# Softmax sums over the partitions inside the layer-1 stages: a transposing reduce on VectorE in place of products with ones on TensorE

## Chip, cores and metric

The kernel runs on one core of a Trainium2 chip. The metric is the device time of one execution in microseconds (us). Every time quoted is a median of runs in the fast state (none more than 1.5% above the fastest of its kernel), unless it is called a profiled span, which is the length of the one execution that the hardware profiler recorded. Six names of engines appear in the profile: PE is TensorE's matmuls, PEld its weight loads, DVE is VectorE, ACT is ScalarE, POOL is GpSimd, and SP is the engine that issues the transfers.

## What is computed

Eight images of 64 channels and 64x64 places pass through two attention layers. In both, every place attends to all 4096 places of its image, and the softmax divides by a sum over all keys. All is fp32.

```python
# layer 0: 8 channels of f and g, 64 of h
s = einsum('bci,bcj->bij', f, g)
o = einsum('bcj,bij->bci', hh, softmax(s, axis=2))
x = x + o
# layer 1: group norm, then q, k, v with 64 channels each
attn = softmax(einsum('bqc,bkc->bqk', q, k) * c ** -0.5)
out = w_proj @ einsum('bqk,bkc->bqc', attn, v) + b_proj
x = out + x
```

## The kernel before

The stages follow one another as layer 0 of image 0, layer 0 of image 1, layer 1 of image 0, layer 0 of image 2, layer 1 of image 1 and so on, each of four chunks of queries. A chunk has 16 steps. A record is one matmul as the profile lists it; an fp32 product appears as two (the four products of one sum are eight records). One step of layer 1 is a group of 16 scores records on TensorE, their exponentials `e` on ScalarE, and a group of 16 that weighs the values by `e` and adds into two accumulators. VectorE adds every `e` into `esum`. The eight PSUM banks are two accumulators (0 and 7) and three pairs that are handed out in turn:

```python
pairs = [banks[:, 2 * k + 1 : 2 * k + 3, :] for k in range(3)]
outer = (0, 7)
def pair():
    ...
    turn += 1
    return pairs[turn % 3]
```

When a chunk has ended, `esum` still holds, on each of 128 partitions, partial sums over different keys. They have to be added over the partitions. Before the change this is done for all of the 64 chunks but the last, so 63 times, by products of a matrix of ones with `esum`:

```python
def finish(self, acc, esum, c, index):
    copied = self.total(raw, acc)       # VectorE copies the accumulators out (layer 1)
    vector.tensor_add(esum[:, 0], esum[:, 0], esum[:, 1])        # 128x1024 is left

    def sums(spare):
        z = banks[:, spare, :] if spare is not None else pair()[:, 0, :]
        for h in range(2):
            for i in range(2):
                row = 32 * (2 * h + i)
                matmul(z[row : row + 32, 0:width], ones[:, 0:32], esum[:, 0, h, ts(i, width)],
                       start=True, stop=True, tile_position=(0, row))
        nc.scalar.copy(zs, z[:, 0:width])
        ...                              # four transfers: one row each, to 32 rows of zt

    def reciprocals():
        vector.reciprocal(rt, zt)        # 128x8, then through HBM to a row for all channels
    ...
# some steps also make a chunk of values for a later stage (64x64 products into a pair);
# VectorE copies them out to vt, which frees the pair
# who runs when: `delay` steps after the end of the chunk
delay = 7 if at.kind == 0 else 5
at_step(now + delay, lambda: sums(spare), PAIR if spare is None else BANK)
at_step(steps[0], behind(reciprocals), 0)        # 3 or 4 steps later; after most layer-0 chunks, in the next layer-1 stage
at_step(steps[1], behind(result), 0)
```

If the next chunk is one of layer 0, the products go to a spare outer bank; inside layer 1 they take a pair in its turn.

Of the kernel before, what the change touches and what calls it, by code (L numbers as in the profile page):

```python
# [9 lines left out]
F32 = mybir.dt.float32  # L10
# [3 lines left out]
ALU = mybir.AluOpType  # L14
AX = mybir.AxisListType
# [5 lines left out]
P = 128  # L21
# [47 lines left out]
def fast_path(  # L69
# [19 lines left out]
    nc = tc.nc  # L89
# [3 lines left out]
    NC = NH // CW  # L93
# [8 lines left out]
    work = ctx.enter_context(tc.tile_pool(name="work", bufs=2))  # L102
# [6 lines left out]
    banks = psum.tile([P, 8, CW], F32, name="banks")  # L109
    pairs = [banks[:, 2 * k + 1 : 2 * k + 3, :] for k in range(3)]  # L110
    outer = (0, 7)
# [3 lines left out]
    def pair():  # L115
        nonlocal turn
        if lent is not None:
            return pairs[lent]
        turn += 1
        return pairs[turn % 3]  # L120
# [26 lines left out]
    vector = InOrder()  # L147

    def matmul(*args, **kwargs):
        in_order(nc.tensor.matmul(*args, **kwargs))  # L150
# [96 lines left out]
    QP = 2 * CW // P  # L247
# [65 lines left out]
    class Attention:  # L313
# [26 lines left out]
        def finish(self, acc, esum, c, index):  # L340

            n = f"{self.name}_{c}"
            raw = work.tile([P, CW], F32, tag="raw", bufs=4, name=f"raw_{n}")
            copied = self.total(raw, acc)
            zt = small.tile([P, QP], F32, tag="zt", bufs=4, name=f"zt_{n}")
            width = CW // 2
            with tc.issue_after(copied.ins if self.kind == 1 else added):
                vector.tensor_add(esum[:, 0], esum[:, 0], esum[:, 1])
            r = None

            def sums(spare):

                if spare is not None:
                    z = banks[:, spare, :]
                else:
                    z = pair()[:, 0, :]

                zs = work.tile([P, width], F32, tag="zs", name=f"zs_{n}")
                for h in range(2):
                    for i in range(2):  # L360
                        row = 32 * (2 * h + i)
                        matmul(
                            z[row : row + 32, 0:width], ones[:, 0:32], esum[:, 0, h, ts(i, width)],
                            start=True, stop=True, tile_position=(0, row),
# [5 lines that stand above are left out]
                        nc.sync.dma_start(zt[row : row + 32, :], zs[row : row + 1, :])  # L370

            def broadcast():
                nonlocal r
                r = work.tile([P, CW], F32, tag="r", name=f"r_{n}")

            def reciprocals():
                rt = stash[:, ts(index, QP)]
                vector.reciprocal(rt, zt)
                broadcast()
                dealt = recips[index]  # L380
                nc.sync.dma_start(dealt, rt)
                for h in range(2):
                    row = dealt[ts(h, C), :].rearrange("p e -> (p e)")
                    nc.sync.dma_start(r[ts(h, C), :], row.partition_broadcast(C))

            def result():
                vector.tensor_mul(raw, raw, r)
                self.residual(raw, c)

            return sums, reciprocals, result  # L390

        def end(self, acc, esum, e, t):

# [49 lines left out]
    class Layer0(Attention):  # L443
        kind = 0
        scale = 1.0
        banks = 1
# [121 lines left out]
    class Layer1(Attention):  # L568
        kind = 1
        scale = C**-0.5  # L570
        banks = 2
# [130 lines left out]
    PAIR, BANK = 1, 2  # L702

    def at_step(s, work_, takes=PAIR):
        nonlocal count
        later.append((s, count, work_, takes))
        later.sort(key=lambda u: u[:2])
        count += 1
# [29 lines left out]
    added = None  # L738
# [20 lines left out]
    def weigh(i, j, e, cols, now):  # L759
        nonlocal acc, esum, first, added  # L760
        at, c = seq[i]
        t, p = divmod(j, 2)
        n = f"{at.name}_{c}"
        if j == 0 and cols.start == 0:
            acc = [banks[:, outer[(c + m) % 2 if at.kind == 0 else m], :] for m in range(at.banks)]
            esum = work.tile([P, 2, 2, CW], F32, tag="esum", name=f"esum_{n}")
        at.weigh(acc, e[:, p], t, p, j == 0, j == 2 * NT - 1, cols)
        if p == 0 or cols.stop < CW:
            return
        if t == 0:  # L770
            first = e
        else:
            added = vector.tensor_add(esum, first if t == 1 else esum, e).ins
        if t == NT - 1:
            finished(i, now)

    def finished(i, now):

        nonlocal closed
        at, c = seq[i]  # L780
        closed = max(closed, 1)
        next_kind = seq[i + 1][0].kind if i + 1 < len(seq) else 1
        works = at.finish(acc, esum, c, i)
        sums, reciprocals, result = works
        delay = 7 if at.kind == 0 else 5
        spare = None
        if next_kind == 0:

            spare = outer[c % 2 if at.kind == 0 else 1]
        if at.kind == 1 and c < NC - 1:  # L790
            spare = None

        at_step(now + delay, lambda: sums(spare), PAIR if spare is None else BANK)

        layer1 = (i // NC + 1) * NC * NT
        if at.kind == 0 and at.b > 0 and c < NC - 1:
            when = layer1 + 1 + 2 * c
            steps = (when, when + 3)
        else:

            wait = 4 if next_kind == 0 else 3
            steps = (now + delay + wait, now + delay + 2 * wait)


        def behind(work_):
            def made():
                with tc.issue_after(added):
                    work_()

            return made  # L810

        at_step(steps[0], behind(reciprocals), 0)
        at_step(steps[1], behind(result), 0)
# [31 lines left out]
    i = 0  # L845
    while i < len(seq):
        at, c = seq[i]
        tight = i < 2 * NC
        if at.kind == 1:
            for j in range(0, 2 * NT, 2):  # L850
                now = i * NT + j // 2
# [21 lines left out]
        while u < len(units):  # L873
            k, t = units[u][:2]
            now = k * NT + t
# [19 lines left out]
            while group:  # L895
# [3 lines left out]
                at, c = seq[k]  # L899
# [12 lines left out]
        i = last  # L912
    now = len(seq) * NT
# [390 lines left out]
```

## Time and profile before

| | before |
|---|---|
| median of 3 runs | 3076.77 us (3076.73 to 3078.01) |
| profiled span, granted TensorE clock | 3076.1 us, 0.998 |
| TensorE, VectorE, ScalarE busy | 99%, 82%, 66% |
| one layer-1 stage, one layer-0 stage | 231.84 us, 147.12 us |

The page's busy line says which engine has no time left, the chain that ended last says whether it also sets the end, and the windows give the same busy times for one stage. What a group costs is read from the timeline, by the differences of starts: matmul groups overlap (in the prediction's timeline groups of 1.97 us start 1.72 us apart), so their durations do not add up. The prediction below shows those views. One more line of the page belongs to the start, the group of the products with ones; its columns are engine, operation, result and operands, shapes, count, then busy us and mean ns of one, then the idle time ahead of them and what ended it.

```profile
L150 PE MATMUL banks<-esum_l,ones 128*32 128x256 f32 x520 | 41.3, 391 | 1.6 <-DVE vt_l L140 1.6
```

These 520 records are 63 sums of 4 products in 2 records each, and 16 records of the last chunk. By this line all 63 sums seem to cost some 40 us. By the starts, the 32 sums that the change touches cost 26.8 us alone.

### The profile page before, as it was taken

To read this page: it belongs to the slowest core of one execution; us is meant where nothing else is said; L and a number is where in the kernel's file an instruction comes from. 1 tells how busy PE (TensorE), PEld (TensorE's weight loads), DVE (VectorE), ACT (ScalarE), POOL (GpSimd) and SP (SyncE) were. 2 spreads that over 40 slices of the span, in tenths; PEclk is the share of its full clock that TensorE was granted. 3 is DMA by queue.
4 is the path that set the end of the run, shared out by engine and by line. 5 is a ranking of instruction groups with operands and counts; after the bars stand their busy time and mean duration, and the time that the engine had idled before them with its cause. 6 is when DMAs were issued, how large, how long until landed. Compare 5 with 4: busy or idle time off the path is not lost.

```text
span 3076.1 us, 59457 instructions
## 1 busy us (share of the span) xinstructions
PE 3047.3 (99%) x26113; PEld 1133.4 (37%) x26113; DVE 2533.3 (82%) x1604; ACT 2045.4 (66%) x2004; POOL 16.4 (1%) x45
## 2 busy tenths in 40 slices
PE   8999999999999999999999999999999999999998
PEld 3333334333343333433334333343333333333433
DVE  6999876899768987689877898779987799876666
ACT  6878655786557865578555785558855588555554
POOL 2000000000000000000000000000000000000000
PEclk9999999999999999999999999999999999999999
DMA  3000010100101001010011000100001000000000
GB/s 78 22 8 12 19 39 15 32 1 15 39 22 25 1 15 39 22 25 1 15 39 26 22 1 18 40 21 22 1 25 36 19 8 1 15 22 15 9 15 13
DMA packets 57531, 62.54 MB, mean 20 GB/s; under 512 B 30816, under 2 KB 30864, under 8 KB 57264
## 3 DMA queue, kind: packets, MB, share of 16 engines
q1 hardware_dynamic: 56272, 58.51, 7.7%
q8 instruction: 206, 3.38, 0.5%
q14 instruction: 61, 0.50, 0.1%
q0 software_dynamic: 672, 0.12, 0.0%
q10 hardware_dynamic: 320, 0.04, 0.0%
HBM read 25.06 MB, written 8.65 MB: 11 GB/s over the span
## 4 chain that ended last, share of the span: by engine, by line
PE 94%; DVE 4%; ACT 1%; issue 1%; DMA 0%; SPq 0%; DVEq 0%; ACTq 0%
PE banks L150 94%; DVE esum_l L140 3%; ACT e_l L902 0%; ACT e_l L861 0%; DVE vt_l L140 0%; DMA x<-in_x_dram 0%; ACT full_l L526 0%; DVE rt L140 0%; DVE w_l L140 0%; DVE x L140 0%; SPq L179 0%; DVE raw_l L140 0%; DVE st_l L140 0%; DVE raw_end L140 0%; DVE guess_l L140 0%
## 5 line engine op out<-in xcount | busy, mean ns | idle before, releaser
L140 DVE TENSOR_TENSOR esum_l<-esum_l,e_l 128x2048 f32<-128x2048 f32 x895 | 2050.2, 2291 | 453.3 <-ACT e_l L861 403.6
L861 ACT ACTIVATE e_l<-banks 128x1024 f32<-128x1024 f32 x1024 | 993.0, 1022 | 800.1 <-PE banks L150 777.8
L150 PE MATMUL banks<-e_l,v_l 64*64 64x512 f32 (+2 forms) x8772 | 1100.4, 588 | 0.0
L902 ACT ACTIVATE e_l<-banks 128x512 f32<-128x512 f32 (+3 forms) x767 | 957.0, 1311 | 193.8 <-PE banks L150 178.2
L150 PE MATMUL banks<-kq_l 64*64 64x512 f32 (+1 forms) x8448 | 1009.5, 586 | 3.4 <-ACT e_l L902 3.2
L150 PE MATMUL banks<-e_l,vt_l 128*64 128x512 f32 (+1 forms) x4060 | 831.7, 550 | 0.0
L150 PEld LDWEIGHTS banks<-e_l,v_l 64*64 64x64 f32 (+1 forms) x8772 | 362.0, 133 | 573.4 <-issue 526.4
L150 PEld LDWEIGHTS banks<-kq_l 64*64 64x64 f32 (+1 forms) x8448 | 348.2, 134 | 578.3 <-issue 542.3
L150 PEld LDWEIGHTS banks<-e_l,vt_l 128*64 128x64 f32 x4060 | 266.9, 136 | 471.4 <-issue 451.4
L150 PE MATMUL banks<-fg_l 32*128 32x512 f32 x1792 | 210.8, 460 | 6.4 <-ACT e_l L902 4.1
L150 PEld LDWEIGHTS banks<-fg_l 32*128 32x128 f32 x1792 | 85.8, 182 | 189.6 <-ACT e_l L902 138.3
L140 DVE TENSOR_TENSOR esum_l<-e_l,e_l 128x2048 f32<-128x2048 f32 x64 | 146.3, 2286 | 6.5 <-ACT e_l L861 6.5
L140 DVE TENSOR_TENSOR esum_l<-esum_l 128x1024 f32<-128x1024 f32 x63 | 76.8, 1220 | 0.9
L140 DVE COPY raw_l<-banks 128x512 f32<-128x512 f32 x31 | 21.4, 692 | 31.3 <-PE banks L150 31.3
L140 DVE TENSOR_TENSOR raw_l<-raw_l,r_l 128x512 f32<-128x512 f32 x63 | 43.1, 684 | 0.0
L150 PE MATMUL banks<-esum_l,ones 128*32 128x256 f32 x520 | 41.3, 391 | 1.6 <-DVE vt_l L140 1.6
L653 ACT ACTIVATE kq_l<-banks,qkb 128x512 f32<-128x512 f32 x64 | 40.7, 697 | 0.0
L150 PE MATMUL banks<-xn_l,wqk 64*64 64x512 f32 x256 | 33.8, 592 | 0.0
L150 PEld LDWEIGHTS banks<-wh,x 64*64 64x64 f32 x1024 | 23.1, 138 | 15.2 <-issue 14.3
L561 ACT COPY raw_l<-banks 128x512 f32<-128x512 f32 x32 | 19.0, 595 | 11.6 <-PE banks L150 11.4
L150 PEld LDWEIGHTS banks<-wvp,xn_l 64*64 64x64 f32 x1024 | 20.6, 134 | 16.4 <-issue 16.4
L140 DVE SCALAR_TENSOR_TENSOR x<-raw_l,hb,x 128x512 f32<-128x512 f32 x32 | 24.0, 751 | 1.1
(109 smaller groups left out, 387.0 us busy)
## 6 DMA issues: line engine op xcount, KB each, us to landing
r_l<-recips SPq DMA_DIRECT2D x126, 128.0 KB, 2.9
fg_l<-high_l SPq DMA_DIRECT2D x216, 64.0 KB, 2.0
kq_l<-kq_l SPq DMA_DIRECT2D x64, 128.0 KB, 2.3
out_dram<-raw_l SPq DMA_DIRECT2D x62, 128.0 KB, 2.4
x<-in_x_dram SPq DMA_DIRECT2D x30, 256.0 KB, 4.7
zt_l<-zs_l SPq DMA_DIRECT2D x252, 1.0 KB, 1.7
kq_l<-high_l SPq DMA_DIRECT2D x32, 64.0 KB, 2.0
recips<-stash SPq DMA_DIRECT2D x63, 4.0 KB, 1.4
```

Of the source, the lines that this page charges most:

```text
L140: it = getattr(nc.vector, name)(*args, **kwargs)
L150: in_order(nc.tensor.matmul(*args, **kwargs))
L561: nc.scalar.copy(raw, acc[0])
L653: nc.scalar.activation(self.parts[:, h, cols], ps[:, h, :], AF.Identity, bias=k1["qkb"][:, h : h + 1],)
L861: nc.scalar.activation(e[:, p], both_ps[p], AF.Exp, scale=at.scale)
L902: nc.scalar.activation(e.rearrange("k p h n -> k (p h) n")[:, first_ : first_ + n_, :], banks[:, bank : bank + n_, :], AF.Exp, scale=at.scale,
```

## The change

TensorE is the bound (busy 99% of the span) and VectorE has idle time in the layer-1 stages (busy 175.70 of 231.84 us). So where the chunk after the one that ended is one of layer 1 (32 of 63 chunks), the sum is made on VectorE. One reduce with a transpose of 32x32 blocks brings 128x1024 down to 128x32 (sums over 32 partitions each), four transfers deal those to 128 rows of four parts, and a small reduce adds the four parts. The products stay where the next chunk is one of layer 0.

```diff
-            r = None
+            r = four = None
+
+            def transposed():
+                nonlocal four
+                both_ = work.tile([P, 8 * QP], F32, tag="zs", name=f"part_{n}")
+                part = both_[:, 0:32]
+                four = both_[:, 32:].rearrange("p (a k) -> p a k", k=QP)
+                with tc.issue_after(added):
+                    vector.tensor_reduce(
+                        part, esum[:, 0].rearrange("p h (i b) -> p b (h i)", b=32),
+                        axis=AX.X, op=ALU.add, apply_transpose=True,
+                    )
+                for a in range(4):
+                    nc.sync.dma_start(four[:, a, :], part[ts(a, 32), :])
 ...
             def reciprocals():
                 rt = stash[:, ts(index, QP)]
+                if four is not None:
+                    vector.tensor_reduce(
+                        zt, four.rearrange("p a k -> p k a"), axis=AX.X, op=ALU.add
+                    )
                 vector.reciprocal(rt, zt)
 ...
-        at_step(now + delay, lambda: sums(spare), PAIR if spare is None else BANK)
+        spare = outer[c % 2 if at.kind == 0 else 1]
+        if next_kind == 1:
+            at_step(now + delay, transposed, 0)
+        else:
+            at_step(now + delay, lambda: sums(spare), BANK)
```

More of the change, by code (lines that the diff above doesn't have):

```diff
@@ L348, in finish @@
                 vector.tensor_add(esum[:, 0], esum[:, 0], esum[:, 1])
-            r = None
+            r = four = None
[11 more added lines that the diff above has]
+                    nc.sync.dma_start(four[:, a, :], part[ts(a, 32), :])
             def sums(spare):
-                if spare is not None:
-                    z = banks[:, spare, :]
-                else:
-                    z = pair()[:, 0, :]
+                z = banks[:, spare, :]
                 zs = work.tile([P, width], F32, tag="zs", name=f"zs_{n}")
@@ L388, in result @@
                 self.residual(raw, c)
-            return sums, reciprocals, result
+            return transposed, sums, reciprocals, result
         def end(self, acc, esum, e, t):
@@ L783, in finished @@
         works = at.finish(acc, esum, c, i)
-        sums, reciprocals, result = works
+        transposed, sums, reciprocals, result = works
         delay = 7 if at.kind == 0 else 5
-        spare = None
-        if next_kind == 0:
-            spare = outer[c % 2 if at.kind == 0 else 1]
-        if at.kind == 1 and c < NC - 1:
-            spare = None
-        at_step(now + delay, lambda: sums(spare), PAIR if spare is None else BANK)
+        spare = outer[c % 2 if at.kind == 0 else 1]
[3 more added lines that the diff above has]
+            at_step(now + delay, lambda: sums(spare), BANK)
         layer1 = (i // NC + 1) * NC * NT
```

## The prediction

> **What bounds the kernel now.** I read the page's busy table first, then the chain that ended last.
>
> ```profile
> PE 3047.3 (99%) x26113; PEld 1133.4 (37%) x26113; DVE 2533.3 (82%) x1604; ACT 2045.4 (66%) x2004; POOL 16.4 (1%) x45
> ...
> PE 94%; DVE 4%; ACT 1%; issue 1%; DMA 0%; SPq 0%; DVEq 0%; ACTq 0%
> ```
>
> TensorE is busy 99% of 3076.1 us and makes up 94% of the chain. VectorE's 4% lies, by the chain in order of time, almost wholly between 143 and 270 us, in the first layer-0 images, which the change does not touch. So a microsecond taken from TensorE's stream in a layer-1 stage is a microsecond of the kernel, and VectorE's 18% of idle time is what the change wants to spend. The change works in layer 1, so I asked for busy times in one whole layer-1 stage (first row) and the layer-0 stage in front of it (second row); columns are length, then busy us of TensorE, its weight loads, VectorE and ScalarE.
>
> ```profile
> 720.92:952.76 231.84, 231.16 (x2372) 88.47 (x2364) 175.70 (x134) 132.64 (x145) 0.00 (x0) 1.00 0.11 27
> 573.80:720.92 147.12, 147.10 (x890) 51.37 (x892) 141.12 (x67) 121.65 (x105) 0.00 (x0) 1.00 0.05 12
> ```
>
> VectorE has 56 us free in a layer-1 stage (76% busy), but only 6 in a layer-0 stage (96%). That is why only chunks whose end is handled inside layer 1 are changed. Next, what one sum by products with ones costs: TensorE alone, in order of time, around one of them.
>
> ```profile
> 1284.37 1.97 PE L150 MATMUL banks<-kq_l 64*64 64x512 f32 x16
> 1286.09 1.97 PE L150 MATMUL banks<-e_l,v_l 64*64 64x512 f32 x16
> 1287.80 1.97 PE L150 MATMUL banks<-kq_l 64*64 64x512 f32 x16
> 1289.71 0.64 PE L150 MATMUL banks<-esum_l,ones 128*32 128x256 f32 x8
> 1290.28 1.95 PE L150 MATMUL banks<-e_l,v_l 64*64 64x512 f32 x16
> 1292.04 1.90 PE L150 MATMUL banks<-kq_l 64*64 64x512 f32 x16
> ```
>
> Read the starts, not the durations. A plain step of layer 1 (scores, then weighing) takes 1287.80 - 1284.37 = 3.43 us; the step with the sums takes 1292.04 - 1287.80 = 4.24 us. The sums therefore cost 0.81 us: 0.19 us more than the usual 1.72 us before they start, 0.57 us for themselves, 0.05 us behind them. Nothing makes it up later: every plain step after it is 3.43 us again.
>
> [...] the six groups above overlap in their durations, and the busy time of a sum (0.64 us) is not its price (0.81). [...] The sums are the one group here with 128x32 tiles between 64x64 ones, and the trace shows a lost 0.11 to 0.19 us ahead and 0.05 behind; projections, which stay at 64x64, show none. [...] in these groups of VectorE by shape (busy, mean ns) a 2048-element add takes 2291 ns and a 1024-element one 1220, so 1.046 ns an element plus 149 ns; 504 elements give 676 ns and the reduce measured 678.
>
> ```profile
> L140 DVE TENSOR_TENSOR esum_l<-esum_l,e_l 128x2048 f32<-128x2048 f32 x895 | 2050.2, 2291 | 453.3 <-ACT e_l L861 403.6 <-DVE esum_l L140 2.3 <-ACT e_l L902 0.9
> L140 DVE TENSOR_TENSOR esum_l<-esum_l 128x1024 f32<-128x1024 f32 x63 | 76.8, 1220 | 0.9
> L140 DVE TENSOR_REDUCE least<-ok 128x1 f32<-128x504 f32 x1 | 0.7, 678 | 0.0
> ```
>
> [...]
>
> **The change part by part.** Which chunks: 8 images x 2 layers x 4 chunks, less the very last, are 63. Those followed by a layer-1 chunk: the last chunk of layer 0 for 7 images, three of each of 8 layer-1 stages (24), and the end of image 6's layer 1, which runs straight into image 7's: 32. Comparing the order of instructions of the two programs confirms it: TensorE loses 32 groups of four products, ScalarE 32 copies of 128x256, VectorE gains 64 reduces, and nothing else changes place on any engine.
>
> *Removed from TensorE.* I took the same difference of starts at all 32 places. It is 0.73 us at 14 of them (0.11 ahead, 0.57, 0.05), 0.81 at 12, and 1.15 at 6. The six are the second chunk of layer 1 of images 0 to 5. One of them:
>
> ```profile
> 849.19 1.97 PE L150 MATMUL banks<-kq_l 64*64 64x512 f32 x16
> ...
> 850.70 0.68 DVE L140 COPY vt_l<-banks 128x512 f32<-128x512 f32 x1
> 851.43 0.16 PEld L150 LDWEIGHTS banks<-esum_l,ones 128*32 128x32 f32 x8 [1.16 <-DVE vt_l L140]
> ```
>
> Scores of 1.72 us should end at 850.9, but the sums start at 851.43. They take the third pair of banks in the rotation, and that still holds the values made a step earlier, which VectorE copies out until 851.38. With the sums gone that pair is next wanted by the first scores of the next step, 849.19 + 3.43 = 852.62, 1.2 us after the copy's end. So I count the stall as gone too. Sum: 14 x 0.73 + 12 x 0.81 + 6 x 1.15 = 10.2 + 9.7 + 6.9 = **26.8 us**, all on the chain.
>
> *Removed from ScalarE.* 32 copies at 0.38 us, 12 us. ScalarE waits for TensorE in these steps, so this is worth nothing.
>
> *Added to VectorE.* 32 transposing reduces of 1024 elements: by the line above 149 + 1024 x 1.046 = 1.22 us (an estimate, as no such instruction has run). 32 reduces of 32 elements to 8: 149 + 33 = 0.18 us. Together 1.4 us x 32 = 45 us. The first stands behind the sum of the step before, where the usual gap is 1.14 us:
>
> ```profile
> 905.20 2.29 DVE L140 TENSOR_TENSOR esum_l<-esum_l,e_l 128x2048 f32<-128x2048 f32 x1 [1.15 <-ACT e_l L861]
> 908.63 2.29 DVE L140 TENSOR_TENSOR esum_l<-esum_l,e_l 128x2048 f32<-128x2048 f32 x1 [1.14 <-ACT e_l L861]
> ```
>
> A 1.22 us piece fits nearly whole; what does not fit is caught up a step later, since each step leaves 1.14 us again. The place without gaps is the start of a layer-1 stage, where VectorE works off layer 0's backlog. There I compared the end of each sum with the start of the ScalarE exponential that refills the same of six buffers: 14 to 16 us of room in layer 1. A delay of 1.4 us stays far inside it. Worth zero.
>
> *Moved.* Four transfers per chunk, formerly 1 KB each from one row, become four of 4 KB that deal 32 rows out to 128. The present ones land in 1.7 us with about 0.6 us of issue each, so some 4 us for four; the second reduce comes three steps, 10.3 us, later. Hidden.
>
> So: 3076.8 - 26.8 = **3050.0 us**, 0.87% less.
>
> **The rivals.** (a) *VectorE becomes the bound in layer 1.* For it: it is the second busiest, and the strided transposing read could run at half rate (2.3 us). Against it: even then 32 x 2.5 = 80 us spread over 8 stages is 10 us in each, of 56 free. TensorE feels VectorE only through copies that free a pair of banks. The tightest is the one above: with the reduce ahead of it at 847.3, at 1.22 us it ends about 851.6, a microsecond early; at 2.3 us it ends about 852.7, and TensorE would wait some 0.1 to 0.2 us, at a handful of places. Cost 0 to 3 us: 3050 to 3053. (b) *The wait for the copy of the values is not removed but moves to the next scores.* Against it stands 1.2 us of room; for it, that the reduce eats part of it. If the whole 0.42 us returned at six places: 3052.5. (c) *The transfers are slow*, since 128 pieces of 32 bytes replace 32, and VectorE, [...] stands at the second reduce. It would have to stand some 14 us before an exponential stalls, though a copy of values behind it could hold TensorE earlier. A microsecond at each of 32 places would make 3070 to 3080; the 10 us of distance speaks against it. (d) *The removed products hid something*, so the gain is only the 0.57 us they take: 18 us, 3058. Against it: the differences of starts already hold the switch of tiles, and steps without sums show none.
>
> **Range and chances.** Most weight lies on the full 26.8 us, as the instruction order is unchanged and the stages repeat to 0.05 us; (a) and (b) stretch upwards, and runs differ by about 1 us. I give 3047 to 3056. A gain of 2% would need 61 us, more than all sums cost; a loss of 2% would need 32 stalls of 2.8 us beyond the gain. Within 2%: 0.98.
>
> **What would show it.** Right: the step with the end of a chunk in layer 1 is 3.43 us like its neighbours; a middle layer-1 stage of 231.84 us shrinks by 3.4; reduces of about 1.2 and 0.2 us; VectorE busier by 45 us, ScalarE less busy by 12; TensorE's wait for the copy of values gone at the six places. Wrong: transposing reduces of 2 us or more, a wait of VectorE for transfers ahead of the small reduce, or new waits of TensorE for the copies of values.

## The result

| | before | after |
|---|---|---|
| median of 4 runs | 3077.39 us (3076.73 to 3078.41) | 3051.35 us (3050.64 to 3054.03) |
| profiled span, clock | 3076.1 us, 0.998 | 3050.3 us, 0.997 |
| a layer-1 stage, a layer-0 stage | 231.84, 147.12 us | 228.51, 147.12 us |
| VectorE busy, ScalarE busy | 2533.3, 2045.4 us | 2596.0, 2036.3 us |

The ratio is 0.9917 (95% interval 0.99 to 0.9934). A ratio here is the mean time of one kernel's runs over that of the other's runs of the same rounds, so it is not quite the ratio of the medians in the table. The change is worth 0.8%, which is within 2%.

The page of the changed kernel: busy times, the chain that ended last, the group of the new reduce, and its transfers (count, KB each, us from issue to landing).

```profile
PE 3023.2 (99%) x25857; PEld 1287.4 (42%) x25857; DVE 2596.0 (85%) x1668; ACT 2036.3 (67%) x1972; POOL 16.7 (1%) x45
...
PE 95%; DVE 3%; issue 1%; ACT 1%; DMA 0%; SPq 0%; DVEq 0%; ACTq 0%
...
L140 DVE TRANSPOSE_TENSOR_REDUCE part_l<-esum_l 128x32 f32<-128x1024 f32 x32 | 63.1, 1973 | 0.0
...
part_l<-part_l SPq DMA_DIRECT2D x128, 4.0 KB, 1.8
```

TensorE is still the bound, with 256 records less (32 groups of 8). The new reduce, 128x32 out of 128x1024 in one instruction, took 1973 ns on average, not 1.22 us, yet VectorE's share of the chain has not grown (3%, against 4% before). PEld rose by 154 us although there are fewer loads; the section on what is missing comes back to it.

The same two stages, by windows: a layer-1 stage and the layer-0 stage in front of it, with length, then busy us of TensorE, weight loads, VectorE and ScalarE.

```profile
717.95:946.46 228.51, 228.10 (x2340) 104.19 (x2333) 183.53 (x142) 131.53 (x141) 0.00 (x0) 1.00 0.11 27
570.83:717.95 147.12, 147.10 (x891) 51.42 (x893) 141.12 (x67) 121.62 (x105) 0.00 (x0) 1.00 0.05 12
```

The layer-1 stage is 3.33 us shorter, and the layer-0 stage has the same length to the hundredth. Four sums fall into such a layer-1 stage: that of the last layer-0 chunk and three of its own. In one of them the whole step looks like this, in the timeline of TensorE and VectorE:

```profile
1275.47 1.99 PE L150 MATMUL banks<-kq_l 64*64 64x512 f32 x16
...
1277.18 1.99 PE L150 MATMUL banks<-e_l,v_l 64*64 64x512 f32 x16
1277.47 1.99 DVE L140 TRANSPOSE_TENSOR_REDUCE part_l<-esum_l 128x32 f32<-128x1024 f32 x1
1278.90 1.99 PE L150 MATMUL banks<-kq_l 64*64 64x512 f32 x16
...
1282.33 1.99 PE L150 MATMUL banks<-kq_l 64*64 64x512 f32 x16
```

From scores to scores the step with the sum takes 1278.90 - 1275.47 = 3.43 us, and the next one, 1282.33 - 1278.90, takes 3.43 us too. TensorE does not notice the sum any more. The same subtraction over all 32 places gives nothing extra at any of them, and 26.8 us less in sum than before.

The tightest place is the second chunk of layer 1, where before the change the products waited for VectorE's copy of the values:

```profile
842.84 1.96 DVE L140 TRANSPOSE_TENSOR_REDUCE part_l<-esum_l 128x32 f32<-128x1024 f32 x1
...
846.89 0.68 DVE L140 COPY vt_l<-banks 128x512 f32<-128x512 f32 x1
847.76 0.23 PEld L150 LDWEIGHTS banks<-kq_l 64*64 64x64 f32 x4 [0.20 <-DVE vt_l L140]
848.18 1.97 PE L150 MATMUL banks<-kq_l 64*64 64x512 f32 x16
```

The copy ended at 847.57 and the scores that overwrite its banks started at 848.18. Although the weight load names the copy as its releaser, its 0.20 us of idle time is what such a load has anyway in this stretch, and the scores start exactly 3.43 us after those before them (844.75). About 0.6 us of room is left.

**What is missing of 26.8 us.** The spans differ by 25.8. Image 1's layer 0, during the start-up of the kernel, begins 0.40 us later in the run after (172.77 against 172.37 us). A second profile of the changed kernel, after_again, has it at 172.25, so two profiles of the same program differ there by more than that. The other part lies at the switches from layer 1 to layer 0. TensorE before, then after, at the same switch:

```profile
947.03 1.90 PE L150 MATMUL banks<-e_l,v_l 64*64 64x512 f32 x16
948.86 0.73 PE L150 MATMUL banks<-fg_l 32*128 32x512 f32 x6
```

```profile
940.64 1.99 PE L150 MATMUL banks<-e_l,v_l 64*64 64x512 f32 x16
942.56 0.73 PE L150 MATMUL banks<-fg_l 32*128 32x512 f32 x6
```

A group of 64x64 tiles usually takes 1.72 us. Ahead of a change of tile shape it took 1.83 us before and takes 1.92 us after. Six such switches cost 0.09 us each more, 0.5 us. The switch goes with the way in which weights are loaded. In the trace the loads of a layer-1 stage come in one of two patterns, 0.15 us busy and 0.28 idle, or 0.23 busy and 0.20 idle (0.24 to 0.25 and 0.18 to 0.19 late in a stage after the change); both fill the same 0.43 us per four loads. Ahead of a change of shape 0.11 us were lost in the first and 0.19 to 0.20 us in the second. Before, each group of products with ones put the loads back into the first pattern; without them the second lasts until the end of the stage, which is the 154 us of PEld. It costs nothing in the plain steps, which take 3.43 us in both. Two of the runs below show that the missing products cause it. In products_kept, the changed kernel with the products put back, the loads return to the first pattern behind each of them, the six switches take 1.82 to 1.83 us again, and PEld's busy time is that of the kernel before:

```profile
PE 3047.7 (99%) x26113; PEld 1134.0 (37%) x26113; DVE 2595.5 (84%) x1668; ACT 2036.6 (66%) x1972; POOL 16.6 (1%) x45
```

In products_64, whose products keep the shape of their neighbours, the switches take 1.90 us and PEld has 1239.8 us. So in these runs the loads returned behind every group of products that changed the shape, and with products that kept it the switches stayed at 1.90 us. They also return without a change of shape: in twice_all, at a place without products, the loads are in the first pattern from 852.11 us on, behind 1.97 us of idle time that ended with the copy of the values, and in products_64 from 854.91 us on, behind 1.16 us of it.

### The profile page after: what moved, and what is told of

Its sections match the earlier page's. It is cut to its first block, busy times and chain, and to the rows that moved or that the text cites. A ratio compares the mean times of both kernels' runs of the same rounds, so it can differ in the third digit from the quotient of the medians.

```text
span 3050.3 us, 58859 instructions
## 1 busy us (share of the span) xinstructions
PE 3023.2 (99%) x25857; PEld 1287.4 (42%) x25857; DVE 2596.0 (85%) x1668; ACT 2036.3 (67%) x1972; POOL 16.7 (1%) x45
## 4 chain that ended last, share of the span: by engine, by line
PE 95%; DVE 3%; issue 1%; ACT 1%; DMA 0%; SPq 0%; DVEq 0%; ACTq 0%
PE banks L150 95%; DVE esum_l L140 3%; ACT e_l L917 1%; DMA x<-in_x_dram 0%; ACT full_l L542 0%; DVE rt L140 0%; DVE w_l L140 0%; DVE x L140 0%; SPq L179 0%; DVE raw_l L140 0%; DVE st_l L140 0%; DVE raw_end L140 0%; DVE guess_l L140 0%; DVE xn_l L140 0%; DVEq L140 0%
## 5 line engine op out<-in xcount | busy, mean ns | idle before, releaser
L150 PE MATMUL banks<-e_l,v_l 64*64 64x512 f32 (+2 forms) x8772 | 1118.2, 588 | 0.0
L150 PE MATMUL banks<-kq_l 64*64 64x512 f32 (+1 forms) x8448 | 1028.3, 586 | 3.4 <-ACT e_l L917 3.2
L150 PEld LDWEIGHTS banks<-e_l,v_l 64*64 64x64 f32 (+1 forms) x8772 | 439.7, 134 | 505.0 <-issue 466.8
L150 PEld LDWEIGHTS banks<-kq_l 64*64 64x64 f32 (+1 forms) x8448 | 422.9, 135 | 503.8 <-issue 468.3
L140 DVE TRANSPOSE_TENSOR_REDUCE part_l<-esum_l 128x32 f32<-128x1024 f32 x32 | 63.1, 1973 | 0.0
```

The lines of the kernel that those rows point to most:

```text
L140: it = getattr(nc.vector, name)(*args, **kwargs)
L150: in_order(nc.tensor.matmul(*args, **kwargs))
```

## The experiments

Eleven kernels ran, in three jobs on three chips; each is compared with runs of the kernel before in its own job. All gave correct results.

### Where the gain comes from

**products_kept.** My theory was that the gain is TensorE's time alone; the rival was that the missing ScalarE copies, or the transfers, matter too. So the changed kernel was given the 32 groups of products back, unread, with no copy by ScalarE.

```diff
+            def products():
+                z = pair()[:, 0, :]
+                ...                       # the four products, as before
             at_step(now + delay, transposed, 0)
+            at_step(now + delay, products, PAIR)
```

> The changed kernel with the 32 groups of products with ones put back on TensorE at their old places, their result read by nobody; no copy by ScalarE, and the sums still come from VectorE. Theory (the gain is TensorE's time alone): the whole gain is lost, 3077 us as before, or up to 3081, because at six places the products must wait for the copy of the values, which now lies about 0.5 us later behind the reduce. Rival (the gain comes from the copies that ScalarE no longer makes, or from the new way of the sums): stays at 3051 to 3060.

It took 3082.31 us (3081.51 to 3083.89) against 3077.9 for the kernel before, ratio 1.0013 (0.9996 to 1.003). The whole gain is gone although ScalarE's busy time stays at 2036.6 us and the sums still take the new way, so nothing of it came from ScalarE or the transfers. The steps cost 0.73 and 0.81 us again, and 1.81 at the second chunk, where the products now wait for a copy that stands behind the reduce:

```profile
848.98 1.99 DVE L140 TRANSPOSE_TENSOR_REDUCE part_l<-esum_l 128x32 f32<-128x1024 f32 x1
...
853.05 0.69 DVE L140 COPY vt_l<-banks 128x512 f32<-128x512 f32 x1
853.80 0.16 PEld L150 LDWEIGHTS banks<-esum_l,ones 128*32 128x32 f32 x8 [1.82 <-DVE vt_l L140]
```

My upper edge was 3081, so the median fell 1.3 us outside of what I had written; the 0.66 us more at six places add up to the 4 us by which the median lies above that of the kernel before, a difference that the ratio's interval does not resolve.

**sums_later.** In the kernel before, the sums of the second chunk were moved two steps back, to a place where the pair they take has long been free. If the extra 0.34 to 0.42 us at the six places is the wait for the copy, it must go.

```diff
-        delay = 7 if at.kind == 0 else 5
+        delay = 7 if at.kind == 0 or c == 1 else 5
```

> The kernel before with the second chunk's sums in each layer 1 two steps later, where the pair of banks in front was not just handed to VectorE's copy of the values. Theory: the stall of 0.42 us at six places goes, and their price falls from 1.15 to 0.73 or 0.81; 2.3 us less than before, 3075.0. Rival (the 0.42 us is a wait for VectorE's sum, or moves to another step): no change, 3077.

The six steps fell from 1.15 us over a plain step to 0.81, the price of the others, and the extra time over the 32 steps with sums from 26.8 to 24.8 us. The run took 3075.83 us (3075.62 to 3077.13), ratio 0.9993 (0.9977 to 1.001): the time alone cannot show 2 us, the trace does. That part of the 26.8 us was thus to be had without VectorE.

**products_64.** What does the change of tile shape cost? In the kernel before, the sums inside layer 1 were made by products in 64x64 tiles over 512 columns, so that no shape changes.

```diff
-                        matmul(z[row : row + 32, 0:width], ones[:, 0:32], esum[:, 0, h, ts(i, width)], ...)
+                            matmul(z[ts(h, C), m, :], ones[ts(m, C), :], esum[ts(m, C), 0, h, :], ...)
```

> The kernel before, with the 32 sums as products with 64x64 tiles like their neighbours: half the rows and 512 columns each, four at once, two partial sums that VectorE adds on 128x8. Theory (of 0.73 to 0.81 us some 0.2 to 0.3 are the changes of tile shape): the four products take 0.43 us, as four scores do, with nothing lost ahead or behind, so 32 x 0.43 + 6 x 0.42 = 16.3 us in place of 26.8: 3066.5. Rival (the lost time ahead and behind is that of any extra group): 32 x (0.43 + 0.2) + 2.5 = 22.7, so 3073.

It took 3083.33 us (3081.96 to 3084.8), ratio 1.0015 (0.9998 to 1.0032), and I had expected 3066.5. The miss was a count of mine: an fp32 product is two records, so these four take 8 x 0.107 = 0.86 us and not 0.43. What the run shows is still of use. At 26 of the 32 places the step costs exactly that 0.86 us: nothing was lost ahead or behind where the shape stayed. At the six second chunks it costs 1.44 us, with a wait for the copy of the values. Products over half the columns would take 0.43 us if the time goes with the columns, an estimate from that 0.86 us; this was not run. By this estimate, of the 0.73 or 0.81 us that one sum cost before, about 0.43 are products and 0.30 to 0.38 are the two changes of tile shape around them. (Inside a group of products with ones the two halves start 0.24 us apart in the trace; counted as 0.48 us of products, that leaves 0.25 to 0.33 for the changes.)

### What the new instruction costs, and whether that matters

**forms.** Five variants, put behind the transposing reduce at some chunks: is it the transpose that takes 1.97 us, or the read with 128 bytes between one element and the next?

```diff
+                        strided = esum[:, 0].rearrange("p h (i b) -> p b (h i)", b=32)
+                        flat = esum[:, 0].rearrange("p h (b x) -> p (h b) x", x=32)
+                        ...    # form 0: plain reduce of strided; 1: plain reduce of flat;
+                        ...    # 2: transposing reduce of flat; 3: transpose of flat; 4: copy of strided
```

> The changed kernel with one further VectorE instruction behind the transposing reduce of the first and third chunk of each layer 1 (results unused), to see why that takes 1.97 us and not 1.22: a strided reduce without transpose, a contiguous reduce, a contiguous transposing reduce, a plain transpose of 128x1024, a strided copy. If the stride costs: strided forms 2 us, contiguous ones 1.22, also the transposing one. If the transpose costs: transposing forms 2 us, strided plain ones 1.22. If both are needed: only the strided transposing one. Time: 3051 to 3055, as these chunks have room for it.

It ran once, in 3053.53 us, so its state is unknown; only durations are used. Groups of VectorE by shape:

```profile
L140 DVE TRANSPOSE_TENSOR_REDUCE part_l<-esum_l 128x32 f32<-128x1024 f32 x32 | 63.2, 1976 | 0.0
...
L140 DVE TENSOR_REDUCE esum_l<-esum_l 128x32 f32<-128x1024 f32 x8 | 12.3, 1541 | 0.0
...
L140 DVE TRANSPOSE_TENSOR_REDUCE esum_l<-esum_l 128x32 f32<-128x1024 f32 x4 | 4.8, 1192 | 0.0
...
L140 DVE STREAM_TRANSPOSE esum_l<-esum_l 128x1024 f32<-128x1024 f32 x2 | 2.4, 1198 | 0.0
```

The second row mixes four strided plain reduces of 1.87 to 1.95 us and four contiguous ones of 1.17 to 1.20. A transposing reduce over contiguous elements took 1.19 us. So in these reduces the transpose cost nothing (1.19 us against 1.17 to 1.20 without it), and the stride some 0.75 us (1.87 to 1.95 us against 1.17 to 1.20; with the transpose, 1976 ns against 1192). The fifth form, a copy of the strided read, took 1.01 and 1.03 us in its two places, where I had expected 2 us, and where the plain reduces of the same read took 1.87 to 1.95. No contiguous copy of the same size ran beside it, so what the stride costs in a copy was not shown.

**twice_all and twice_but_second.** If VectorE's extra time were near to being the bound, doubling it would show. The first kernel does every transposing reduce twice; the second does so everywhere but at the second chunk of layer 1, where the copy of the values has only 0.6 us of room.

```diff
+                    if True:            # twice_but_second: if not (self.kind == 1 and c == 1)
+                        again = esum[:, 1, 0, 0:32]
+                        vector.tensor_reduce(again, ..., apply_transpose=True)   # the same read
```

> The changed kernel with every transposing reduce done twice (the second result unused): 32 x 1.97 = 63 us more for VectorE. Theory (VectorE is off the path but for one copy of values): the copy that frees the pair of banks for the scores of the second chunk ends 0.6 us before they start, so 1.97 us more makes them 1.4 us late at six places: 8.3 us more, 3060; every other step of layer 1 unchanged. Rival (VectorE is near to bounding layer 1): losses at other chunks too, 3070 to 3110. Third (it has room everywhere): 3051.

> As before, but the reduce of the second chunk of each layer 1 done once: 24 x 1.97 = 47 us more for VectorE. Theory: no step gets longer, 3051.4 as the changed kernel (within 1.5). Rival (VectorE near to bounding layer 1): about three quarters of what doing all twice costs.

twice_all took 3060.86 us (3059.97 to 3061.31), the 3060 of the theory, ratio 0.9943 (0.9926 to 0.996). twice_but_second took 3051.71 us (3051.1 to 3053.91), ratio 0.9916 (0.9899 to 0.9932), the ratio of the change itself. So 24 more reduces, by which VectorE was 43.7 us busier, cost nothing, and 8 at the one tight place cost 9 us. Of these, 8.3 us stand in six layer-1 stages, each 229.90 us long in place of 228.52. In twice_all that place reads:

```profile
846.86 1.94 DVE L140 TRANSPOSE_TENSOR_REDUCE esum_l<-esum_l 128x32 f32<-128x1024 f32 x1
...
850.90 0.68 DVE L140 COPY vt_l<-banks 128x512 f32<-128x512 f32 x1
...
851.63 0.21 PEld L150 LDWEIGHTS banks<-kq_l 64*64 64x64 f32 x8 [1.97 <-DVE vt_l L140]
```

The scores are due at 846.85 + 3.43 = 850.28 and start at 851.63. This is the wait of rival (b) of the prediction. It exists, and begins some 0.6 us beyond what the change asks for.

### Can more sums be moved?

Thirty-one sums by products are left. Those of layer-0 stages I did not try on VectorE where they are, as it is 96% busy there.

**held_l0.** The halved sums of the first three chunks of layer 0, images 2 to 7 (18 sums), are held in a buffer that is free then, and reduced at the start of the next layer-1 stage.

```diff
+        if at.kind == 0 and at.b >= 2 and c < NC - 1:
+            slot = c                    # vector.tensor_add writes into the held buffer
-        if next_kind == 1:
+        if slot is not None:
+            start = (i // NC + 1) * NC * NT + 2 * slot
+            at_step(start, transposed, 0)
+        elif next_kind == 1:
```

> The changed kernel, with 18 more sums taken from TensorE: those of the first three chunks of layer 0 of images 2 to 7. Their halved sums are held in the still unused buffer of the image's own layer 1 and reduced by VectorE at the beginning of the next layer-1 stage, where it has room, not in layer 0, where it is 96% busy. Theory (each sum is TensorE's time on the path in layer 0 too): at least 18 x 0.57 = 10 us, up to 16 with the steps that needn't keep a bank free: 3035 to 3041. Rival (layer 0 is held by VectorE, so the freed time becomes waiting for exponentials' buffers): 3048 to 3052. Rival 2 (the work at the start of layer 1 delays the statistics that TensorE needs there): up to 3060.

It took 3057.28 us (3054.99 to 3059.53), ratio 0.9935 (0.9918 to 0.9951), slower than the change and far from the 3035 to 3041 of the theory. The gain is there: the layer-0 stages fell from 147.12 to between 144.55 and 145.02 us, at best 0.86 us for each of three sums. But the layer-1 stages behind them rose from 228.51 to between 231.15 and 231.40 us, one to 233.28. At the end of their first chunk TensorE waits for VectorE's copy of the accumulators:

```profile
769.18 1.04 PE L150 MATMUL banks<-x,wfg 64*64 64x512 f32 x8
772.08 2.30 PE L150 MATMUL banks<-e_l,v_l 64*64 64x512 f32 x14 [1.86 <-DVE raw_l L140]
```

I had looked at the exponential buffers and at the copy of the values, and overlooked this third dependence: the next chunk's first weighing overwrites the accumulators, and VectorE reaches their copy only when it has worked off layer 0's backlog and what was put ahead, 57.3 us into the stage against 53.5 in the change.

**held_all.** The same with layer 1's last chunk also held, 24 sums fewer on TensorE.

```diff
+        elif at.kind == 1 and next_kind == 0:
+            slot = 3
```

> As the kernel with held sums of layer 0, and also the last chunk of layer 1 of images 0 to 5, held over the whole layer-0 stage behind it: 24 sums less than in the changed kernel. Theory: at least 24 x 0.57 = 13.7, up to 21 us: 3030 to 3038. Rivals: as there; VectorE gets five reduces at the start of each layer-1 stage, about 10 us, so a wait of TensorE for the statistics or for the next image's input would show near the first third of the stage.

It took 3090.07 us (3089.5 to 3090.73), ratio 1.004 (1.0023 to 1.0056), slower than the kernel before, where I had expected 3030 to 3038. Its granted clock was 0.991, against 0.997 for the change. The five layer-1 stages concerned took about 239 us, and the same place shows why:

```profile
776.24 4.47 PE L150 MATMUL banks<-e_l,v_l 64*64 64x512 f32 x16 [7.23 <-DVE raw_l L140]
```

The wait is not all of the 10 us. By the windows of this trace, the granted clock fell from 1.00 to 0.50 while TensorE waited, at 771.4 us, and rose again only at about 781.5 us. The group behind the wait started 3.46 us before the next one in place of 1.72. In held_l0, with 1.86 us of waiting, the windows show 1.00 throughout.

**held_spread, with after_again as control.** If that copy is the cause, the held sums must be free when their work is spread over the stage. The third held reduce starts two steps later. The results of the third and of the last layer-0 chunk, and the statistics of the layer, were moved behind the end of the first chunk; the projections and values that follow start five steps later.

```diff
-            at = [18, 22, 26] if self.b == 0 else [16, 20, 24]
+            at = [18, 22, 26] if self.b == 0 else [16, 20, 24] if self.b == 1 else [22, 25, 29]
-            start = (i // NC + 1) * NC * NT + 2 * slot
+            start = (i // NC + 1) * NC * NT + (0, 2, 6)[slot]
+            first_step = (i // NC + 1) * NC * NT + 8 if at.kind == 0 and at.b >= 2 else now + delay
+                steps = (layer1 + 12, layer1 + 21)
 ...                                    # the values and projections, five steps later
```

> The changed kernel itself, beside the two that follow, on the same chip: 3051 us, 0.992 of before.

> The 18 held sums of layer 0 again, but the work they bring to layer 1 is spread: the third chunk's reduce at step 6, its result and the last chunk's only behind the end of the first layer-1 chunk, and the statistics and projections that follow three to five steps later. The run with held sums at the start lost 2.3 us and more in each stage where TensorE waited at a chunk's end for VectorE to copy the accumulators. Theory (that wait was the only loss, and the layer-0 stage keeps its gain of 2.6 us in each of 6 stages): 3051 - 15 = 3036. Rival (layer 0 gains, but the same work of VectorE costs TensorE elsewhere in layer 1): 3040 to 3052.

The control took 3052.56 us (3050.86 to 3053.84), ratio 0.9918 (0.9902 to 0.9935): the result repeats. held_spread took **3038.83 us** (3037.28 to 3039.95), ratio 0.9871 (0.9854 to 0.9887), so it beats both kernels. The layer-0 stages keep their 144.6 to 145.0 us and the layer-1 stages are back at 228.57 us (one at 228.86). The copy of the accumulators starts 53.5 us into the stage, as in the change, and not 57.3 as in held_l0. TensorE at the same place no longer waits for it:

```profile
771.80 1.04 PE L150 MATMUL banks<-x,wfg 64*64 64x512 f32 x8
772.66 1.90 PE L150 MATMUL banks<-e_l,v_l 64*64 64x512 f32 x16
```

**held_dealt.** A last attempt at the stride: the halving sum writes its result dealt out, so that the held reduce can read contiguously.

```diff
+                        cut.rearrange("p (b h i) -> p h i b", b=32, h=2),      # result of the sum
-                        part, halved.rearrange("p h (i b) -> p b (h i)", b=32),
+                        ... else cut.rearrange("p (b x) -> p b x", b=32),
```

> As the spread one, with the halving sum of the held chunks writing its result already dealt out, so that the transposing reduce reads it in order, which took 1.19 us in place of 1.97. If a strided write costs nothing (1.22 us for that sum): VectorE gains 18 x 0.78 = 14 us in layer 1, no change of the time, 3036. If it costs as a strided read does (about 2 us), VectorE loses 0.8 us three times in each layer-0 stage, where it has least room: 3036 to 3042.

It took 3052.3 us (3050.24 to 3055.14), ratio 0.9915 (0.9899 to 0.9932): the further gain of held_spread is lost, and the time lies outside of the 3036 to 3042 that I gave. Its groups of VectorE by shape, then those of held_spread:

```profile
L140 DVE TENSOR_TENSOR kq_l<-esum_l 128x1024 f32<-128x1024 f32 x18 | 35.9, 1994 | 0.6
...
L140 DVE TRANSPOSE_TENSOR_REDUCE kq_l<-kq_l 128x32 f32<-128x1024 f32 x18 | 22.3, 1237 | 0.0
```

```profile
L140 DVE TENSOR_TENSOR kq_l<-esum_l 128x1024 f32<-128x1024 f32 x18 | 22.0, 1224 | 0.6
```

The stride cost as much in the write (1994 against 1224 ns, 0.77 us) as in the read (1973 against 1192 ns, 0.78 us), and the write stands in the layer-0 stages, where VectorE has no room; these grew to 146.0 to 148.6 us. That is 2.5 us more in a stage on average, for three writes that are 0.77 us longer: what was free in layer 1 was paid in full in layer 0.

## Why the prediction was right, and where a term was off

- **The bound and the gain.** The prediction said 26.8 us off TensorE's stream and 3050.0 us. The steps gave back 26.8 us, and the median was 3051.35. That TensorE's time is all of it is shown by products_kept, and that the spans differ by 25.8 is accounted for above: 0.5 us at the switches of layer, which the prediction did not have, and 0.4 us of scatter in the start-up.
- **Rival (d), that only 0.57 us of each sum come back,** would have given 3058, and fell. Differences of starts hold the changes of shape, some 0.3 us by the estimate from products_64.
- **"By the line above 149 + 1024 x 1.046 = 1.22 us"** is the term that was mis-sized. The transposing reduce took 1.97 us, so VectorE grew by 62.7 us and not 45 (32 x (1.973 + 0.201) = 69.6; instructions back to back overlap by about 0.08 us in the trace, as 842.84 + 1.96 against the next start at 844.72, which takes off some 5, and the 895 large adds measured 1.5 less). The sum was fitted to contiguous reads. The prediction did name the strided read as a risk, at 2.3 us (twice the fitted time an element, 149 + 2 x 1024 x 1.046 ns), in rival (a), and "transposing reduces of 2 us or more" as a sign of being wrong, which 1.93 to 2.00 us all but met; the time came out right because the room at the tightest place was enough for it. By the trace an element of the strided read took (1973 - 149) / 1024 = 1.78 ns, an estimate with the 149 ns of the prediction's fit, against the fit's 1.046; no such reduce runs in the kernel before, so its trace gave no better size.
- **"A delay of 1.4 us stays far inside it. Worth zero."** This held at 2 us also, and at 4 us everywhere but at one place (twice_but_second).
- **Rivals (a) and (b), new waits of TensorE for the copy of the values,** did not appear, but with 0.6 us to spare, not the microsecond that was told. twice_all shows the wait that they describe.
- **Rival (c), slow transfers,** did not appear. The transfers landed in 1.8 us and no small reduce waited for one.
- **The wait at the six second chunks** was for the pair that held the values, as the prediction said; sums_later removes it without the change.
- **ScalarE** fell by 9 us, predicted 12, and was worth nothing, as predicted.

What stays open is why the weight loads of layer 1 come in two patterns, and why ScalarE fell by 9 us and not by 12.

## What to carry to other kernels

Price a group on the bounding engine by the differences of starts around it: its busy time said 0.64 us here, and it cost 0.73 to 1.15. Work moved to VectorE, idle 18% of the span before, was free here only where it did not stand in front of something that TensorE waited for; these were the copies out of PSUM, and the same 18 held sums lost some 5 us when all their work stood ahead of such a copy (ratio 0.9935 against the 0.9917 of the change) and gained 14 us when part of it was moved behind. Look at how an access pattern steps, not only at which operation runs: a stride of 128 bytes took a reduce from 1.2 to 2.0 us, which was free in one stage and ate the gain in another. A sum over the partitions was made without TensorE here by a transposing reduce over blocks of 32 (1.97 us strided, 1.19 us contiguous), four transfers of 1.8 us and a reduce of 0.2 us.
